# Routing scores of two tiles per strip on VectorE, and four row buffers instead of five

## The chip, the cores and the metric

The kernel runs on one core of one Trainium2 chip. The metric is the device time of one launch in microseconds (us). Three runs of the kernel before gave 1011.37, 1012.25 and 1013.17 us, so the median is 1012.25 us. The profile comes from one further execution, which took 1011.34 us; the span that the profile covers in it is 1009.5 us.

The engines of a core work side by side, each through its own instructions in order: TensorE (PE in the profile; PEld is its weight load) multiplies matrices into PSUM, VectorE (DVE) and ScalarE (ACT) work elementwise, GpSimd (POOL) here mostly issues DMAs, and SyncE (SP) issues DMAs from a queue of its own. An engine waits for another through semaphores. SBUF is the memory that the engines work from.

## The reference, cut to what matters

One layer of a graph network over 3125 nodes with 256 features: a layer norm, a GNN branch with sparse products, an attention-like mix, and then a mixture of eight experts with one expert for each node. What the change touches is the routing: the second layer norm's output times an 8-column matrix, from which each node's expert is picked.

```python
xn = _layernorm(x, axis=-1)
x = x + gnn(xn, ...) + mix(xn, ...)
h = _layernorm(x, axis=-1)
logits = h @ gate_w + gate_b          # [3125, 256] @ [256, 8]
idx = argmax(softmax(logits))
pos = rank of the node among those with the same idx
buf[idx, pos] = h                     # 489 slots for each expert
y = relu(buf @ w1 + b1) @ w2 + b2     # then back to the nodes
out = x + y * probability
```

The GNN branch is `h = A x`, then `z = A h` and a softmax, then `A` times that result and a second softmax. `A` is the sparse 3125 x 3125 matrix, which the kernel builds as a dense one in HBM (`adj`).

## The kernel before

**Stages.** The first stage builds `adj` from the edge lists (until about 248 us). Then come three dense products with it: the first with the normed input (two column halves, until about 515 us), the second with `g` (until about 682 us), the third with `late`, the softmax of the second (until about 831 us). Behind the third product come the experts (until about 1001 us).

**The products.** Each product runs over seven strips of target nodes, `STRIPS`: five of four tiles (512 columns), one of three (384) and one of two (181 real columns). A strip takes 25 chunks of source nodes, one matmul each per column half (`multiply`, L275; fp32, so that the trace has two records for one matmul). The chunks' rows come from HBM in loads of five chunks, 1280 KB for a strip of 512 columns. `load_part` (L250) takes a buffer `at` from `apool` (L772, five buffers of 10 KB per partition) and issues the load on SyncE's queue; so a load waits until TensorE is done with the buffer that it takes over, and SyncE's later instructions wait behind it.

**The strip's tail.** In the third product, TensorE's order is written by hand (L1436 to L1482). While strip s+1 is multiplied, `tail(s)` (L1285), a generator, is advanced between the loads' stretches of five chunks, at the places 0, 2, 3 and 4 of `at` in L1440:

- place 0: the strip's sum is copied (ACT), turned by `w1T` (L1306, PE). Then VectorE and ScalarE do the second softmax, tanh and the sum `x` (L1313 to L1337); the sum lies in `rows`, whose first half is the lower 128 features (done earlier) and the other half the upper 128.
- place 2: TensorE transposes the upper half of each tile (L1343), ScalarE copies the result to `xT` (L1344).
- place 3: TensorE multiplies each turned tile by the upper half of the gate, `gate_c[:, 1, :]`, 8 columns (L1348).
- place 4: VectorE has computed the layer norm's mean and scale (L1353 to L1358, `inv_sqrt` at L115 with three Newton steps), the logits (L1360, sum of TensorE's result and `g_lo`), the choice `oh` (L1372 to L1376) and the running counts `run` (L1379). TensorE then ranks the nodes with two matmuls on `run` and `oh` (L1383, L1384). These stand in TensorE's order ahead of the next strip's chunks.

After that VectorE computes the row numbers (L1398 to L1402), GpSimd scatters the tokens to `xbuf` (L1411) and SyncE writes `x` to `out` (L1424). After strip 3's tail `early_experts` (L1077) picks the two fullest experts, which begin before the last strips are through; their numbers are read by SyncE and GpSimd (L1105, L1459).

**The lower half of the gate** is done on VectorE already, beside the second product: `gate_lo` (L956) holds the gate's rows, spread over all partitions, less their mean; `gate_tile` (L968) multiplies a tile by it into `dot` (L970, 128 x 1024 elements) and sums over the features into `g_lo` (L973). `spread_gate` (L959) loads the rows by a DMA on GpSimd's queue and subtracts the mean (L963).

**Memory.** Pools are laid out as stacks from both ends of SBUF, and a tile that takes over the place of an older one waits for that one's last readers. `hT` (L775, 25 KB per partition, the first product's result) lies above `apool`, and the tiles of the tails come down from the other end as far as its place. TensorE's last reads of `hT` are the transposes at L1013 at the end of the second product. All engines but TensorE in the third product, and all of them in the second, are in the order that the scheduler gives when it builds the program.

Of the kernel before, what the change touches and what calls it, by code (L numbers as in the profile page):

```python
# [8 lines left out]
FP = mybir.dt.float32  # L9
# [3 lines left out]
ALU = mybir.AluOpType  # L13
AX = mybir.AxisListType
PSUM = bass.MemoryType.PSUM

P = 128
N = 3125
D = 256
HD = 128  # L20
# [5 lines left out]
STRIPS = [(0, 4), (4, 4), (8, 4), (12, 4), (16, 4), (20, 3), (23, 2)]  # L26
# [20 lines left out]
NEXP = 8  # L47
# [21 lines left out]
def rows_all(ap, offset, n):  # L69

    return bass.AP(tensor=ap.tensor, offset=ap.offset + offset, ap=[[0, P], [1, n]])
# [3 lines left out]
def gps_layer(ctx: ExitStack, tc: tile.TileContext, a: dict, out: bass.AP):  # L75
    nc = tc.nc
# [8 lines left out]
    small = ctx.enter_context(tc.tile_pool(name="small", bufs=3))  # L85
# [9 lines left out]
    def mm():  # L95
        mm_pools.append(mm_pools.pop(0))
        return mm_pools[-1].tile([P, SW], FP, tag="mm", name="mm")
# [256 lines left out]
    def network(runs):  # L354

        with ExitStack() as net:
            layer(net, runs)

    def layer(net, runs):
# [409 lines left out]
        gnn = net.enter_context(ExitStack())  # L769
        zpool = gnn.enter_context(tc.tile_pool(name="zpool", bufs=2))  # L770
        parts = gnn.enter_context(ExitStack())
        apool = parts.enter_context(tc.tile_pool(name="apool", bufs=5))  # L772
        held_h = parts.enter_context(ExitStack())
        hold = held_h.enter_context(tc.tile_pool(name="hold", bufs=1))
        hT = hold.tile([P, 2, NP], FP)  # L775
# [8 lines left out]
        if runs:  # L784
# [3 lines left out]
        w0T, w1T, b0, b1, gate_b, gate_c, gate_m, g_lo, ones = (  # L788
            held[x]
            for x in ("w0T", "w1T", "b0", "b1", "gate_b", "gate_c", "gate_m", "g_lo", "ones")  # L790
        )
# [202 lines left out]
        for s, (t0, nt) in enumerate(STRIPS):  # L994
# [12 lines left out]
            for j in range(0, nt, 2):  # L1007
                m = min(2, nt - j)
                t = t0 + j
                pt = mm()  # L1010
# [12 lines left out]
            x = xa[:, t0 : t0 + nt, :HD]  # L1023
# [257 lines left out]
        routing = net.enter_context(ExitStack())  # L1281
        strip = routing.enter_context(tc.tile_pool(name="strip", bufs=2, side="right"))
        rpool = routing.enter_context(tc.tile_pool(name="rpool", bufs=3, side="right"))

        def tail(s, p):  # L1285

            t0, nt = STRIPS[s]
            tiles = slice(t0, t0 + nt)

            def st(tag):  # L1290
                return small.tile([P, 4, NEXP], FP, tag=tag, name=tag)[:, :nt, :]
# [4 lines left out]
            def wide_(v):  # L1296
                return v[:, :, None].to_broadcast([P, nt, NEXP])
# [29 lines left out]
            x = rows[:, :, :D]  # L1327
# [9 lines left out]
            nc.vector.tensor_tensor(x[:, :, HD:], xa[:, tiles, HD:], s1, ALU.add)  # L1337


            xT = strip.tile([P, SW], FP, tag="xT", name="xT")  # L1340
            pt = mm()
            for j in range(nt):
                nc.tensor.transpose(pt[:, j * P : (j + 1) * P], x[:, j, HD:], ident)  # L1343
            nc.scalar.copy(xT[:, : nt * P], pt[:, : nt * P])  # L1344
            yield
            pg = mm()
            for j in range(nt):
                nc.tensor.matmul(  # L1348
                    pg[:, j * NEXP : (j + 1) * NEXP], xT[:, j * P : (j + 1) * P], gate_c[:, 1, :],
                    start=True, stop=True,  # L1350
                )
            yield
            mv = small.tile([P, 4, 2], FP, tag="mv", name="mv")[:, :nt, :]  # L1353
            for j in range(nt):
# [3 lines left out]
            inv_sqrt(rs, mv[:, :, 1], nt)  # L1358
            logit = st("logit")
            nc.vector.tensor_tensor(  # L1360
                logit, pg[:, : nt * NEXP].rearrange("p (t e) -> p t e", e=NEXP), g_lo[:, tiles, :],
                ALU.add,
            )
            nc.vector.tensor_tensor(logit, logit, wide_(rs), ALU.mult)
            nc.vector.tensor_tensor(
                logit, logit, gate_b[:, None, :].to_broadcast([P, nt, NEXP]), ALU.add
# [41 lines left out]
            for j in range(nt):  # L1408
                t = t0 + j
# [26 lines left out]
        with tc.manual_schedule(engines={mybir.EngineType.PE}):  # L1436
            behind = iter(())
            end = len(STRIPS) - 1
            for s in range(len(STRIPS)):
                at = (0, 2, 3, 4) if s < end else (0, 4)  # L1440
                (p,) = spmm(
                    s, lambda c, d: s0[:, c, :], 1,
                    lambda i: next(behind, None) if i % (NT // CH) in at else None,
                )
                if s < end:
                    for _ in behind:
                        pass
                    behind = tail(s, p)
                if s == EARLY_AT + 1 and runs:
                    early, num, row, full, low = early_experts()  # L1450
            last = tail(end, p)
            parts.close()
            wts = net.enter_context(tc.tile_pool(name="wts", bufs=2))
# [55 lines left out]
            if runs:  # L1509
# [9 lines left out]
                right = ranked.tile([1, 1], FP, name="right")  # L1519
# [187 lines left out]
```

## Time and profile before

| what | value |
|---|---|
| median of three runs | 1012.25 us |
| the profiled execution | 1011.34 us |
| its span in the profile | 1009.5 us |
| TensorE in the 150 us from 700 to 850 us | busy 149.9 us |
| VectorE there | busy 68.7 us of 150 |
| DMA engines there, in stretches of 50 us | 0.92, 0.90 and 0.94 busy |
| TensorE's clock as granted | 0.993 of full speed on average |

The columns of the profile's tables are explained where they are shown. In a row of instruction groups the duration of one matmul is longer than the time from its start to the next one's start, because matmuls overlap; the chain of waits has the time that each really adds. An engine's idle time before an instruction stands in brackets, with what ended it. The profile marks a queue's own waiting with a q (SPq).

### The profile page before, as it was taken

The numbers are of one execution on the slowest core, as the hardware profiler recorded it, in microseconds if no ns is written. First come the engines' busy times: TensorE is split into PE (matmuls) and PEld (weight loads), VectorE is DVE, ScalarE is ACT, GpSimd is POOL, SyncE is SP. The second block draws the span as 40 slices with busy tenths as digits, with TensorE's granted clock in tenths as the row PEclk, the third lists the DMA queues.
The fourth block names the chain that finished last, engine by engine and source line by source line (L and its number), as shares of the span: only waits on it lengthen the run. The fifth ranks groups of instructions, "written<-read, shape, count | busy, mean of one in ns | idle before, by whom it ended". The sixth has DMA issues, their size and how long they took to land.

```text
span 1009.5 us, 11457 instructions
## 1 busy us (share of the span) xinstructions
PE 977.7 (97%) x4202; PEld 635.9 (63%) x4202; DVE 514.5 (51%) x1149; ACT 304.5 (30%) x567; POOL 98.3 (10%) x113
## 2 busy tenths in 40 slices
PE   5889999999999999999999999999999999999996
PEld 3878888854444444455665554474444578888995
DVE  7999799800343444445653675575444465221211
ACT  3889889830000001001101001110111133224431
POOL 6511000000000000000000000000011142111111
PEclk7999999999999999999999999999999999999999
DMA  4989888993933247421475658769999797713300
GB/s 134 258 240 261 239 238 239 254 263 113 340 116 104 98 139 209 133 75 54 125 243 198 218 196 269 235 182 374 314 310 301 250 320 244 234 36 125 107 30 21
DMA packets 171641, 197.94 MB, mean 196 GB/s; under 512 B 7664, under 2 KB 118304, under 8 KB 171575
## 3 DMA queue, kind: packets, MB, share of 16 engines
q1 hardware_dynamic: 164285, 178.56, 56.6%
q0 software_dynamic: 7248, 18.51, 6.4%
q8 instruction: 35, 0.57, 0.2%
q14 instruction: 31, 0.25, 0.1%
q10 hardware_dynamic: 42, 0.05, 0.0%
HBM read 144.43 MB, written 53.37 MB: 196 GB/s over the span
## 4 chain that ended last, share of the span: by engine, by line
PE 85%; DMA 4%; DVE 4%; ACT 3%; issue 2%; SPq 1%; POOL 0%; POOLq 0%; ACTq 0%; DVEq 0%
PE acc L275 48%; PE mm L1205 7%; PE acc L1162 7%; PE acc L654 5%; PE b L654 5%; PE mm L833 4%; PE mm L889 2%; DMA adj<-st_rows 2%; PE pk L861 1%; ACT st_rows L658 1%; ACT rhs L639 1%; PE mm L916 1%; DMA at<-adj 1%; PE mm L1013 1%; PE mm L1306 1%
## 5 line engine op out<-in xcount | busy, mean ns | idle before, releaser
L275 PE MATMUL acc<-at,xn 128*128 128x512 f32 (+3 forms) x540 | 203.2, 523 | 1.3 <-DMA at<-adj 1.3
L275 PEld LDWEIGHTS acc<-at,xn 128*128 128x128 f32 (+1 forms) x540 | 96.4, 190 | 89.3 <-issue 75.1
L275 PE MATMUL acc<-at,g 128*128 128x512 f32 (+4 forms) x350 | 137.8, 541 | 0.0
L275 PE MATMUL acc<-at,late 128*128 128x512 f32 (+4 forms) x350 | 137.4, 543 | 0.0
L275 PEld LDWEIGHTS acc<-at,late 128*128 128x128 f32 (+1 forms) x350 | 62.4, 190 | 59.6 <-issue 54.1
L275 PEld LDWEIGHTS acc<-at,g 128*128 128x128 f32 (+1 forms) x350 | 62.9, 190 | 58.6 <-issue 52.3
L654 PE MATMUL acc<-rhs,lhs 128*125 128x128 f32 x626 | 85.7, 280 | 9.4 <-ACT rhs L639 8.5
L626 DVE TENSOR_TENSOR lhs<-in_row,in_blk 128x1000 f32<-128x1000 f32 (+1 forms) x79 | 90.3, 1183 | 1.2
L654 PEld LDWEIGHTS acc<-rhs,lhs 128*125 128x125 f32 x626 | 77.5, 191 | 20.9 <-ACT rhs L639 10.2
L654 PE MATMUL b<-rhs,lhs 128*125 128x128 f32 x624 | 81.9, 275 | 0.0
L654 PEld LDWEIGHTS b<-rhs,lhs 128*125 128x125 f32 x624 | 75.4, 190 | 0.0
L639 ACT CAST rhs<-cells 128x2048 f32<-128x2048 bf16 x39 | 74.9, 1920 | 0.2 <-DVE cells L617 0.2
L275 PE MATMUL acc<-a,xn 128*128 128x512 f32 (+1 forms) x160 | 73.1, 595 | 1.2 <-DMA a<-adj 1.1
L846 ACT ACTIVATE sq<-kv 128x512 f32<-128x512 f32 x25 | 15.8, 630 | 179.4 <-DVE kv L842 179.4
L1205 PE MATMUL mm<-w,hm 128*128 128x256 f32 (+2 forms) x288 | 64.3, 380 | 0.0
L839 DVE TENSOR_REDUCE kmean<-mm 128x8 f32<-128x512 f32 x25 | 17.3, 691 | 91.6 <-PE mm L833 91.6
L1162 PE MATMUL acc<-xeT,w 128*128 128x208 f32 (+2 forms) x288 | 58.9, 361 | 1.6 <-ACT hm L1166 0.9
L1205 PEld LDWEIGHTS mm<-w,hm 128*128 128x128 f32 (+2 forms) x288 | 51.2, 180 | 9.6
L1162 PEld LDWEIGHTS acc<-xeT,w 128*128 128x128 f32 x288 | 53.0, 190 | 5.7 <-ACT hm L1166 1.3
L658 ACT COPY st_rows<-acc 125x512 f32<-125x512 f32 (+1 forms) x79 | 47.6, 603 | 25.0 <-issue 14.5
L1166 ACT ACTIVATE hm<-acc,b_e 128x256 f32<-128x256 f32 (+2 forms) x72 | 32.4, 455 | 66.7 <-PE acc L1162 66.5
L617 DVE TENSOR_TENSOR cells<-steps_w,edge_h 128x2048 bf16<-128x2048 bf16 (+1 forms) x40 | 47.7, 1192 | 4.6 <-ACT rhs L639 4.4
(271 smaller groups left out, 1037.8 us busy)
## 6 DMA issues: line engine op xcount, KB each, us to landing
at<-adj SPq DMA_DIRECT2D x52, 1280.0 KB
adj<-st_rows SPq DMA_DIRECT2D x39, 896.0 KB
at<-adj SPq DMA_DIRECT2D x14, 1024.0 KB
at<-adj SPq DMA_DIRECT2D x12, 960.0 KB
w<-in_f_w SPq DMA_DIRECT2D x10, 1024.0 KB
a<-adj SPq DMA_DIRECT2D x39, 256.0 KB
at<-adj SPq DMA_DIRECT2D x12, 452.5 KB
adj<-st_rows SPq DMA_DIRECT2D x39, 104.0 KB
```

The costliest lines, as they stand in the source:

```text
L275: nc.tensor.matmul(ps[d][:, :w], stationary(c, d)[:k], a_rows[:k, :w], start=(c == 0), stop=(c == NT - 1),)
L617: nc.vector.tensor_tensor(cells[:, :m, :, :k], steps_w[:, None, :, :k].to_broadcast([P, m, P, k]), of_pairs(1, g0, ng, P), ALU.is_equal,)
L626: nc.vector.tensor_tensor(lhs[:, j::k], in_row[:, j::k, :, None].to_broadcast([P, m, GR, CA]), in_blk[:, :, None, :, j].to_broadcast([P, m ...
L639: nc.scalar.copy(rhs.rearrange("p (i j) c -> p i j c", j=2), cells.rearrange("p i c j -> p i j c"),)
L654: nc.tensor.matmul(p[:GP, j * P : (j + 1) * P], lhs[:, j0 + j], rhs[:, j0 + j], start=True, stop=True,)
L658: nc.scalar.copy(st[:GP, j0 : j0 + nj, :], p[:GP, : nj * P].rearrange("p (g b) -> p g b", b=P),)
L833: nc.tensor.matmul(pkv, xnT[:, d, t * P : (t + 1) * P], w_kv[:, d, :], start=(d == 0), stop=(d == 1),)
L839: nc.vector.tensor_reduce(mean, p3, AX.X, ALU.add)
L889: nc.tensor.matmul(p[:, j * D : (j + 1) * D], xnT[:, d, (t0 + j) * P : (t0 + j + 1) * P], w_mix[:, d, :], start=(d == 0), stop=(d == 1),)
L1162: nc.tensor.matmul(p[:, :slots], w1[:, d, f * P : (f + 1) * P], xeT[:, d, :slots], start=(d == 0), stop=(d == 1),)
L1166: nc.scalar.activation(hm[:, f, :slots], p[:, :slots], AF.Relu, bias=b1_e[:, f : f + 1], scale=1.0)
L1205: nc.tensor.matmul(p[:n, :D], hm[:, f, c : c + n], w2[:, f, :], start=(f == 0), stop=(f == FC - 1),)
```

## The change

In the first five strips (s from 0 to 4) the last two of the four tiles no longer go through TensorE for the upper half of the gate. VectorE multiplies each of them by `gate_hi`, the upper gate rows spread over all partitions, into a buffer `dot_2`, sums over the features into `part`, and adds that to `g_lo`. TensorE transposes and multiplies the other two tiles only, `xT`'s copy is half as wide, and the logits of two tiles come from PSUM and of two by a copy of `g_lo`. The last two strips keep TensorE for all their tiles.

`gate_hi` and the buffer that holds first the raw rows and then each `dot_2` are two tiles of 4 KB per partition in a new pool; the raw rows (4 KB for each partition, 512 KB) are loaded by one DMA on GpSimd's queue. To make room, `apool` has four buffers instead of five.

```diff
-        apool = parts.enter_context(tc.tile_pool(name="apool", bufs=5))
+        apool = parts.enter_context(tc.tile_pool(name="apool", bufs=4))
...
+        by_rows = routing.enter_context(tc.tile_pool(name="by_rows", bufs=1, side="right"))
+        gate_hi = by_rows.tile([P, NEXP, HD], FP)
+        raw = by_rows.tile([P, HD, NEXP], FP, tag="dot", name="gate_rows_2")
+        nc.gpsimd.dma_start(raw, rows_all(a["gate_w"], HD * NEXP, HD * NEXP).rearrange(
+            "p (d e) -> p d e", e=NEXP))
+        nc.vector.tensor_tensor(
+            gate_hi, raw.rearrange("p d e -> p e d"),
+            gate_m[:, :, None].to_broadcast([P, NEXP, HD]), ALU.subtract,
+        )
...
+            mt = nt - 2 if s < len(STRIPS) - 2 else nt
+            for j in range(mt, nt):
+                dot = by_rows.tile([P, NEXP, HD], FP, tag="dot", name="dot_2")
+                nc.vector.tensor_tensor(
+                    dot, gate_hi, x[:, j, None, HD:].to_broadcast([P, NEXP, HD]), ALU.mult
+                )
+                part = small.tile([P, NEXP], FP, tag="part", name="part")
+                nc.vector.tensor_reduce(part, dot, AX.X, ALU.add)
+                nc.vector.tensor_tensor(g_lo[:, t0 + j, :], g_lo[:, t0 + j, :], part, ALU.add)
             xT = strip.tile([P, SW], FP, tag="xT", name="xT")
             pt = mm()
-            for j in range(nt):
+            for j in range(mt):
                 nc.tensor.transpose(pt[:, j * P : (j + 1) * P], x[:, j, HD:], ident)
-            nc.scalar.copy(xT[:, : nt * P], pt[:, : nt * P])
+            nc.scalar.copy(xT[:, : mt * P], pt[:, : mt * P])
             yield
             pg = mm()
-            for j in range(nt):
+            for j in range(mt):
                 nc.tensor.matmul(
...
             nc.vector.tensor_tensor(
-                logit, pg[:, : nt * NEXP].rearrange("p (t e) -> p t e", e=NEXP), g_lo[:, tiles, :],
-                ALU.add,
-            )
+                logit[:, :mt, :], pg[:, : mt * NEXP].rearrange("p (t e) -> p t e", e=NEXP),
+                g_lo[:, t0 : t0 + mt, :], ALU.add,
+            )
+            if mt < nt:
+                nc.vector.tensor_copy(logit[:, mt:, :], g_lo[:, t0 + mt : t0 + nt, :])
```

What the built program shows of the order: the first product is ordered as before on TensorE. Between the second and the third product, TensorE's order before has one matmul of the third product ahead of the last transposes (L999, L1013); in the changed program that matmul stands behind them. The subtraction into `gate_hi` stands on VectorE between two steps of the second product's last softmax (L140 and L141). In the tails of the strips 0 to 4 the four new large instructions stand on VectorE behind `x` and among the statistics, ahead of `inv_sqrt`. On SyncE's queue the load of each stretch comes one buffer later against TensorE's progress, and the first write of `x` stands one load earlier in the order. GpSimd has one more DMA, ahead of the first tail's work.

## The prediction

> **What bounds the kernel now.** I read the engines' busy times first, then the chain of waits in two tails of the third product, then VectorE's timeline of the last of them, then the stretch between second and third product.
>
> ```profile
> PE 977.7 (97%) x4202; PEld 635.9 (63%) x4202; DVE 514.5 (51%) x1149; ACT 304.5 (30%) x567; POOL 98.3 (10%) x113
> ```
>
> TensorE is busy for 97% of the span, so work taken from it counts one to one where nothing else becomes late. The chain of waits beside strip 1, for the tail of strip 0 (start, length, engine, line, count of records):
>
> ```profile
> 719.05 0.44 PE mm L1343 x4
> 719.49 4.29 PE acc L275 x10
> 723.78 0.79 PE mm L1348 x8
> 724.57 4.59 PE acc L275 x10
> 729.16 0.34 PE mm L1383 x2
> ```
>
> The chain stays on TensorE, which waits for nobody: the tail's small matmuls only take its time. The same in the tail of strip 4, which lies beside strip 5 (384 columns):
>
> ```profile
> 814.16 0.44 PE mm L1343 x4
> 814.60 3.23 PE acc L275 x10
> 817.83 0.79 PE mm L1348 x8
> 818.62 3.52 PE acc L275 x10
> 822.14 0.34 PE mm L1383 x2
> ```
>
> From the transposes to L1383 it is 10.1 us in the first and 8.0 us in the second: VectorE has 2.1 us less there.
>
> **Gain on TensorE.** Half of L1343 (0.44 / 2 = 0.22 us) and half of L1348 (0.79 / 2 = 0.40 us) leave each of five strips: 0.62 us a strip, 3.1 us in all. I take the chain's times, since matmuls overlap and the durations of their group rows would count the overlap too.
>
> **What VectorE gets.** Two multiplies, two sums and two small adds a strip, and a small copy. The lower half of the gate shows the same operation on the same shape:
>
> ```profile
> 679.85 1.22 DVE L970 TENSOR_TENSOR dot<-gate_lo,xa 128x1024 f32<-128x1024 f32 x1
> 681.11 1.22 DVE L973 TENSOR_REDUCE g_lo<-dot 128x8 f32<-128x1024 f32 x1
> ```
>
> The starts are 1.26 us apart, so four cost 4.9 to 5.0 us, and the adds, which go between the statistics, some 0.1 each. From x to the start of the Newton steps (L120) VectorE now takes 1.29 us; with the four it takes about 6.0, or 4.7 more. They stand ahead of L120 in VectorE's order, so the statistics, the Newton steps, the logits, the choice and the counts `run` all queue behind them, and TensorE waits for `run` at L1383, with the next strip's chunks behind it.
>
> *Strips 0 to 3.* In strip 0 x is ready at 716.41 (VectorE's timeline). Plus 6.0, plus 2.4 for the Newton steps, plus the 2.5 from the logits' first step to the last count: `run` at about 727.3. TensorE comes to L1383 at 729.16 less 0.62, or 728.5. So 1.2 us are left, no wait arises, and the gain is whole: 4 x 0.615 = 2.46 us.
>
> *Strip 4.* VectorE's timeline:
>
> ```profile
> 813.04 0.69 DVE L1337 TENSOR_TENSOR rows<-xa,s 128x512 f32<-128x512 f32 x1 [0.75 <-issue]
> ...
> 815.06 0.17 DVE L120 TENSOR_SCALAR nv<-mv 128x4 f32<-128x4 f32 x1
> ...
> 817.47 0.17 DVE L1387 COPY rows<-rs 128x4 f32<-128x4 f32 x1
> ...
> 818.65 0.19 DVE L1360 TENSOR_TENSOR logit<-mm,g_lo 128x32 f32<-128x32 f32 x1 [0.95 <-PE mm L1348]
> 818.88 0.19 DVE L1364 TENSOR_TENSOR logit<-logit,rs 128x32 f32<-128x32 f32 x1
> ...
> 820.72 0.55 DVE L1379 TENSOR_TENSOR run<-run,oh 128x8 f32<-128x8 f32 x3
> ```
>
> Before, VectorE itself waited 0.95 us for TensorE's gate. Now: x ends at 813.77, L120 comes at 813.77 + 6.0 = 819.8, the Newton steps end 817.47 - 815.06 = 2.4 later at 822.2, and from L1364 to the last count before TensorE's ranking is 821.07 - 818.88 = 2.2: `run` at 824.4. TensorE is there at 822.14 - 0.62 = 821.5. It **waits 2.9 us** for VectorE, which becomes the bound at this one place. What is saved in strip 4 goes with it: +2.9 - 0.6 = +2.3 us.
>
> **Does a wait of 2.9 us cost the clock?** What the trace shows of the throttle is the granted clock in 3.4-us windows (window, length, busy PE, PEld, DVE, ACT and POOL, PEclk, DMA share, GB/s):
>
> ```profile
> 9.90:13.30 3.40, 0.41 (x2) 0.20 (x2) 1.65 (x8) 0.34 (x1) 3.09 (x3) 1.00 0.22 43
> 13.30:16.70 3.40, 0.91 (x2) 0.36 (x2) 2.60 (x5) 1.59 (x3) 2.79 (x3) 0.50 0.70 187
> 44.00:47.40 3.40, 1.59 (x15) 1.40 (x14) 3.30 (x8) 3.13 (x4) 3.06 (x2) 1.00 1.06 311
> ```
>
> After a window with TensorE busy for 0.41 us the clock fell to 0.50; after one busy for 1.59 us it stayed at 1.00. The wait, if it fell wholly into one window, would leave 0.5 us of work, near the first row: half clock for at least one window, some 1.7 us. [...] I take 0 for the sum and keep 1.7 as a case.
>
> **Between second and third product.** TensorE before (timeline):
>
> ```profile
> 676.39 6.19 PE L275 MATMUL acc<-at,g 128*128 128x181 f32 x38
> 682.51 1.12 PE L275 MATMUL acc<-at,late 128*128 128x512 f32 x2
> 683.47 0.38 PE L999 MATMUL mm<-ident,zT 128*128 128x128 f32 x2
> 683.69 0.60 PE L1013 MATMUL mm<-ident,hT 128*128 128x128 f32 x4
> 684.12 2.31 PE L275 MATMUL acc<-at,late 128*128 128x512 f32 x5
> ```
>
> One matmul of the third product (0.96 us until L999) filled the wait for `zT`, which ScalarE copies from 682.67 to 683.08. In the new order L999 and L1013 stand ahead of it: TensorE is idle from 682.4 to 683.15, the third product starts at about 683.8 with 25 chunks instead of at 684.12 with 24. A chunk is 0.86 us: 683.8 + 0.86 - 684.12 = **+0.54 us**.
>
> **Four buffers.** The tight place is the same. Loads before were issued at 675.89, 677.81, 679.35, 680.88 and 682.61 and landed at 681.0, 684.4, 687.9, 691.3 and 694.3, 3.4 us apart: the DMA engines are the limit there.
>
> ```profile
> 685.00:690.00 5.00, 5.00 (x13) 2.27 (x12) 4.39 (x11) 0.83 (x2) 0.00 (x0) 1.00 1.05 385
> ...
> 695.00:700.00 5.00, 5.00 (x13) 2.14 (x12) 0.21 (x1) 0.00 (x0) 0.00 (x0) 1.00 1.06 331
> ```
>
> (Columns as in the last fence.) With four buffers the same releases serve one load further back: the third product's first load is issued at 677.81 and lands at 683.0 to 683.4, needed at 683.8; the second at 686.5, needed 688.1; the third at 690.0, needed 692.4; the fourth at 693.5, needed 696.7. No stall, with 0.5 us to spare at the first: from below nothing, from above the 3.4 us of a load that misses its place. I take 0, since landings 3.4 us apart are faster than the 4.3 us that five chunks take. Later in the product three loads are on the way for 12.9 us while one takes 5 to 8 us. The earlier products have the same margin: 0.
>
> **The gate's rows.** The added DMA moves 512 KB to where the share is 1.05: at 385 GB/s that is 1.4 us on the loads behind it (third load at 691.4, still ahead of 692.4). It starts once `hT` is read (L1013, about 684). For its like, L961, issue to VectorE's start took 522.8 - 515.7 = 7.1 us, and the subtraction 2.01, so `gate_hi` is done at 694. VectorE's softmax between L140 and L141 waits for it; TensorE needs that last `late` tile at chunk 23, about 703.6. Nine microseconds of chunks cover it: 0, and without that cover all that is over 9 us. SyncE's first write of x now stands one load earlier and moves it by some 2 us, with 17 to spare; GpSimd's queue is empty there.
>
> **Sum.** -2.46 + 2.3 + 0.54 = +0.4, rounded up to +0.5 for the small adds. On the profiled 1011.34 that is 1011.8; the median lies 0.9 higher, which gives **1012.7 us**. Of this kernel a change of 0.2%, 2.0 us, can be told from none.
>
> **The rivals.**
> *Clock drop after strip 4's wait.* For: the 9.90 row. [...] Price 1.7 less the overlap: +2.0 in all, 1014.2 us.
> *Loads starve.* The other side, slower: with four buffers the first load or the third is late, because the rows for the gate interleave with it ahead of the gap that I assume. It decides from 0.5 us of delay at the first load and 1.0 at the third; from there each load is late by what it lacks, at most 3.4 us for one. For: share 1.05. Against: the landings. +2 to +5, 1013.2 to 1017, middle 1015.
> *VectorE is in time.* The scheduler's order would let the small steps overlap, or x would be ready earlier because TensorE's front part is shorter; if strip 4 waited 0.6 us only, so that it gains nothing, and the boundary lost nothing: -2.46, 1009.8 us. Against: the four instructions alone are 4.9 us against 0.95 of slack and what lies ahead of it.
> *The change does not do what it says*, because the scheduler puts the four behind L120: excluded by the built order.
>
> **How the numbers follow.** Forecast 0.40, clock 0.27, in time 0.17, starving 0.16. The range runs from the third rival's 1009.8 to inside the starving case: 1009.7 to 1016; the likeliest's own is 1011.7 to 1014. Faster by over 0.2% is the third rival, 0.17; slower takes the starving case, the clock case and a little of the forecast's upper end, 0.46; within 0.2% the rest, 0.37.
>
> **What would show it.** L1343 and L1348 at half count in five strips; TensorE idle ahead of L1383 by 2.5 to 3.3 us in strip 4 alone, released by VectorE L1379; PEclk of the next windows; a gap of 0.7 us ahead of L999; no wait of a third-product matmul for `at`. Wrong would be waits at L1383 in strips 0 to 3 (up to 5 x 2 us if x came late), or TensorE idle for loads.

## The result, and the profile after

The changed kernel takes 1017.8 us (median of ten runs, 1016.5 to 1022.08) against 1012.09 us for the kernel before beside it: a ratio of 1.006 (95% interval 1.005 to 1.0071), so **5.7 us slower**. A second measurement on another chip gave 1016.82 against 1013.55, ratio 1.0036 (1.0021 to 1.0052). The prediction was 1012.7 with a range up to 1016.

The profiled execution took 1018.02 us, its span is 1016.4 us. The first row is the page's line of engines, the second its group of the third product's matmuls, whose last part is the idle time just before them and what ended it:

```profile
PE 978.6 (96%) x4172; PEld 636.6 (63%) x4172; DVE 537.8 (53%) x1185; ACT 304.1 (30%) x567; POOL 97.8 (10%) x114
...
L275 PE MATMUL acc<-at,late 128*128 128x512 f32 (+4 forms) x350 | 139.5, 550 | 1.5 <-DMA at<-adj 1.4
```

TensorE has 30 records fewer and yet 0.9 us more of busy time: part of the work ran at a lower clock (0.50 in the windows shown below). And it waited 1.4 us for rows of the matrix, which it had not done before. The view of the waits on TensorE from 680 to 840 us (what waited, for what: sum, times, longest) names all that are new; the same view of the kernel before, from 680 to 835 us, is empty:

```profile
PE mm L1406 <- DVE run L1402: 2.8, 1, 2.8
PE acc L275 <- DMA at<-adj: 1.4, 2, 0.8
PE mm L999 <- ACT zT L983: 0.6, 1, 0.6
```

(L1406 is the ranking that was L1383 before; L1402 was L1379, and L1364, L1369 were L1343, L1348.) Where these stand is seen in TensorE's timelines. From the second to the third product, and to the start of its second strip:

```profile
679.06 6.19 PE L275 MATMUL acc<-at,g 128*128 128x181 f32 x38
685.81 0.44 PE L999 MATMUL mm<-ident,zT 128*128 128x128 f32 x2 [0.57 <-ACT zT L983]
686.09 0.60 PE L1013 MATMUL mm<-ident,hT 128*128 128x128 f32 x4
687.44 21.92 PE L275 MATMUL acc<-at,late 128*128 128x512 f32 x50 [0.75 <-DMA at<-adj]
709.96 4.56 PE L275 MATMUL acc<-at,late 128*128 128x512 f32 x10 [0.60 <-DMA at<-adj]
```

The order is the forecast one, with L999 ahead of the first `late` chunk, but two loads come late. Without the first of them the product would start at 686.69, 1.44 us behind the end of the second (685.25), with 25 chunks to go; before it was 1.54 us (682.58 to 684.12) with 24. One chunk being 0.86 us, the order costs 1.44 + 0.86 - 1.54 = 0.76 us. The start of the first tail (L1306 before, now L1317) gives what this whole stretch loses:

```profile
709.41 1.05 PE L1306 MATMUL mm<-w1T,zT 128*128 128x128 f32 x8
714.35 0.83 PE L1317 MATMUL mm<-w1T,zT 128*128 128x128 f32 x6
```

From the end of the second product it was 26.83 us (709.41 - 682.58) and is 29.10 (714.35 - 685.25). Of the 2.27 us, 0.76 are the order, so late loads cost 1.5. That is more than the 1.35 us of idle time that the two rows show: at the second wait the starts of the matmuls lie 0.75 us further apart than elsewhere and 0.60 are shown as idle, since the matmul ahead is still running by the profile. VectorE's own wait for the gate's rows stands beside it:

```profile
694.72 2.01 DVE L1291 TENSOR_TENSOR gate_hi<-gate_rows,gate_m 128x1024 f32<-128x1024 f32 x1 [3.89 <-DMA gate_rows<-in_gate_w]
```

In strip 4's tail:

```profile
820.09 3.87 PE L275 MATMUL acc<-at,late 128*128 128x384 f32 x10
826.77 0.60 PE L1406 MATMUL mm<-run,ones 128*128 128x32 f32 x2 [2.81 <-DVE run L1402]
827.19 0.61 PE L1407 MATMUL mm<-oh,upto 128*128 128x32 f32 x2
827.62 3.37 PE L275 MATMUL acc<-at,late 128*128 128x181 f32 x10
```

The wait is there. Before, the same ten records of 181 columns took 1.78 us:

```profile
822.54 1.78 PE L275 MATMUL acc<-at,late 128*128 128x181 f32 x10
```

Now they take 3.37: they run at half clock. VectorE's timeline ahead of it, in the changed kernel:

```profile
815.33 0.69 DVE L1348 TENSOR_TENSOR rows<-xa,s 128x512 f32<-128x512 f32 x1 [0.75 <-issue]
816.06 1.23 DVE L1355 TENSOR_TENSOR dot<-gate_hi,rows 128x1024 f32<-128x1024 f32 x1
...
817.40 1.20 DVE L1359 TENSOR_REDUCE part<-dot 128x8 f32<-128x1024 f32 x1
...
820.27 1.21 DVE L1359 TENSOR_REDUCE part<-dot 128x8 f32<-128x1024 f32 x1
...
822.05 0.17 DVE L120 TENSOR_SCALAR nv<-mv 128x4 f32<-128x4 f32 x1
...
826.28 0.55 DVE L1402 TENSOR_TENSOR run<-run,oh 128x8 f32<-128x8 f32 x3
```

From x (816.02) to L120 it is 6.0 us, and VectorE does not pause until `run`. The table by windows (window, length, busy PE, PEld, DVE, ACT, POOL, granted clock, DMA share, GB/s) shows the clock:

```profile
823.00:826.42 3.42, 0.91 (x2) 0.29 (x2) 3.04 (x24) 0.72 (x2) 0.00 (x0) 1.00 1.06 384
826.42:829.83 3.41, 3.06 (x11) 3.09 (x12) 1.04 (x7) 0.00 (x0) 0.26 (x1) 0.50 0.87 275
829.83:833.24 3.41, 3.41 (x14) 3.41 (x14) 0.91 (x2) 0.00 (x0) 2.80 (x3) 0.50 0.37 77
833.24:836.65 3.41, 3.41 (x24) 3.41 (x24) 1.33 (x6) 2.20 (x8) 1.20 (x3) 1.00 0.99 227
```

After a window with TensorE busy for 0.91 us, two windows were at half clock. By this reading half of the busy time in them, (3.06 + 3.41) / 2 = 3.2 us, is lost; e3 measures it.

### The profile page after: what moved, and what is told of

Read it like the earlier page. It is cut to its first block, busy times and chain, and to the rows that moved or that the text cites. A ratio compares the mean times of both kernels' runs of the same rounds, so it can differ in the third digit from the quotient of the medians.

```text
span 1016.4 us, 11441 instructions
## 1 busy us (share of the span) xinstructions
PE 978.6 (96%) x4172; PEld 636.6 (63%) x4172; DVE 537.8 (53%) x1185; ACT 304.1 (30%) x567; POOL 97.8 (10%) x114
## 5 line engine op out<-in xcount | busy, mean ns | idle before, releaser
L275 PE MATMUL acc<-at,xn 128*128 128x512 f32 (+3 forms) x540 | 202.9, 523 | 1.5 <-DMA at<-adj 1.5
L275 PEld LDWEIGHTS acc<-at,xn 128*128 128x128 f32 (+1 forms) x540 | 96.6, 190 | 89.1 <-issue 75.1
L275 PE MATMUL acc<-at,late 128*128 128x512 f32 (+4 forms) x350 | 139.5, 550 | 1.5 <-DMA at<-adj 1.4
L275 PE MATMUL acc<-at,g 128*128 128x512 f32 (+4 forms) x350 | 137.8, 541 | 0.0
L275 PEld LDWEIGHTS acc<-at,late 128*128 128x128 f32 (+1 forms) x350 | 64.6, 196 | 61.7 <-issue 52.5
L275 PEld LDWEIGHTS acc<-at,g 128*128 128x128 f32 (+1 forms) x350 | 62.9, 190 | 58.6 <-issue 52.3
L275 PE MATMUL acc<-a,xn 128*128 128x512 f32 (+1 forms) x160 | 73.1, 595 | 1.7 <-DMA a<-adj 1.6
L1234 DVE SCALAR_TENSOR_TENSOR y<-mm,xe,bx 128x256 f32<-128x256 f32 (+2 forms) x22 | 10.6, 482 | 78.7 <-PE mm L1205 74.3
```

Source lines behind the costliest of these rows:

```text
L275: nc.tensor.matmul(ps[d][:, :w], stationary(c, d)[:k], a_rows[:k, :w], start=(c == 0), stop=(c == NT - 1),)
L1234: nc.vector.scalar_tensor_tensor(y, p[:n, :D], xe[:n, j, D + 2 : D + 3], bx, op0=ALU.mult, op1=ALU.add, accum_out=row_sums[:n, k : k + 1],)
```

## The experiments

**How they are compared.** The first stage, the same in every kernel, ends at times that differ by 4 us from profile to profile. So beside each ratio stands the *third product's length*: from the end of the second product's last matmul to the end of the third's last one, read from TensorE's records of L275. In four kernels whose third product is not slowed (before, e5, e8, e12) it is 148.74 to 148.78 us.

| kernel | ratio to before (95% interval) | first product starts at, us | third product, us |
|---|---|---|---|
| before | 1 | 252.42 | 148.74 |
| changed | 1.0060 (1.0050 to 1.0071) | 255.14 | 153.89 |
| e14, changed again | 1.0036 (1.0021 to 1.0052) | 256.02 | 153.92 |
| e5, before again | 1.0000 (0.9989 to 1.0011) | 253.27 | 148.74 |
| e1, four buffers alone | 1.0071 (1.0054 to 1.0088) | 256.02 | 153.49 |
| e2, strip 4 on TensorE | 1.0047 (1.0029 to 1.0065) | 254.62 | 152.52 |
| e3, wait filled | 1.0037 (1.0021 to 1.0052) | 255.53 | 151.14 |
| e4, last rows split | 1.0037 (1.0024 to 1.0049) | 254.10 | 152.42 |
| e6, weights later | 1.0050 (1.0037 to 1.0063) | 255.35 | 153.98 |
| e7, split and strip 4 on TensorE | 1.0006 (0.9995 to 1.0017) | 254.33 | 148.94 |
| e8, five buffers, split | 1.0000 (0.9990 to 1.0010) | 252.57 | 148.74 |
| e9, fifth's place kept | 1.0071 (1.0050 to 1.0092) | 256.52 | 152.98 |
| e10, four buffers, split | 1.0026 (1.0012 to 1.0041) | 255.26 | 153.11 |
| e11, e7 with later writes | 0.9992 (0.9979 to 1.0004) | 256.38 | 147.96 |
| e12, five buffers, later writes | 0.9999 (0.9981 to 1.0016) | 254.78 | 148.78 |
| e13, five buffers, added matmuls | 1.0021 (1.0003 to 1.0038) | 255.60 | 150.90 |

Both profiles of the changed kernel have a third product 5.2 us longer than before, which lies in both intervals of the ratio (5.1 to 7.2 and 2.1 to 5.3 us).

**e3: is the clock a cost of its own?** Ahead of strip 4's ranking:

```diff
+            if s == len(STRIPS) - 3:
+                pf = mm()
+                for k in range(5):
+                    nc.tensor.matmul(
+                        pf[:, : mt * P], ident, xT[:, : mt * P], start=(k == 0), stop=(k == 4)
+                    )
             p3 = mm()[:, : nt * NEXP].rearrange("p (t e) -> p t e", e=NEXP)
```

> The changed kernel with five matmuls on data at hand (256 columns each, their result is not used) ahead of strip 4's ranking, in the time in which TensorE waits for VectorE. The wait's end is not moved. Theory (the clock is a cost of its own, since TensorE idles 2.5 us of one window): about 0.7 us of idle time are left, the clock stays 1.00, and the kernel is 3.4 us faster than the changed one, about 1014.4. Rival (the clock's fall is incidental or hides behind other work): same time as the changed kernel.

TensorE's timeline:

```profile
824.35 2.43 PE L1408 MATMUL mm<-xT,ident 128*128 128x256 f32 x10
827.43 0.38 PE L1412 MATMUL mm<-run,ones 128*128 128x32 f32 x2 [0.65 <-DVE run L1402]
827.64 0.39 PE L1413 MATMUL mm<-oh,upto 128*128 128x32 f32 x2
827.87 1.78 PE L275 MATMUL acc<-at,late 128*128 128x181 f32 x10
```

The wait's end is where it was against `x`, the granted clock stays 1.00, and the ten records take 1.78 us again. The third product is 2.75 us shorter, although the second strip's first load came 0.47 us later than in the changed kernel (1.07 against 0.60). Together 3.2 us, what the two windows lost. e13 prices the filler where nothing waits: the same five matmuls with five buffers.

> Five buffers and nothing of the change; five matmuls whose result is not used stand ahead of strip 4's ranking. With five buffers, too, the first product starts at 252.4 to 253.3 if the buffers decide, or elsewhere if each program has a start of its own. The time: 2.1 us above before for the added matmuls.

It took 150.90 - 148.74 = 2.16 us more in the third product. So matmuls that cost 2.2 us elsewhere bring 2.75 us here: the clock's loss is shown.

**e2: strip 4 left on TensorE.**

```diff
-            mt = nt - 2 if s < len(STRIPS) - 2 else nt
+            mt = nt - 2 if s < len(STRIPS) - 3 else nt
```

> The changed kernel, with strip 4 left wholly on TensorE (VectorE's part in strips 0 to 3 only). Theory (the wait of 2.8 us in strip 4 and two windows of half clock behind it are the largest loss): no wait ahead of L1406, clock 1.00 through the third product, 2.8 + 3.4 - 0.7 = 5.5 us faster than the changed kernel, so about 1012.3 and the same as before. Rival (buffers and loads are the larger loss): 2 us faster than the changed kernel at most, about 1016.

The third product is 1.4 us shorter, not 5.5; the ratio is that of the rival. The wait ahead of the ranking is gone, but another one stood behind it. TensorE's timeline:

```profile
823.83 0.41 PE L1406 MATMUL mm<-run,ones 128*128 128x32 f32 x2
824.08 0.39 PE L1407 MATMUL mm<-oh,upto 128*128 128x32 f32 x2
826.71 3.14 PE L275 MATMUL acc<-at,late 128*128 128x181 f32 x10 [2.24 <-DMA at<-adj]
```

The last strip's first load is 2.24 us late, and one window of half clock follows. In the changed kernel VectorE's wait lay over it, and both ended together: the ranking started at 826.77, and the trace's semaphore records have the last step of that load at 826.85. **Two causes, each enough to stop TensorE at this place.**

**e1: four buffers alone.**

```diff
-        apool = parts.enter_context(tc.tile_pool(name="apool", bufs=5))
+        apool = parts.enter_context(tc.tile_pool(name="apool", bufs=4))
```

> The kernel before with four row buffers and nothing else of the change. Theory (a load lands only when the slowest of its 16 parts has landed, and four buffers give no room for that): TensorE waits about 0.6 us ahead of L999, 0.7 us for the first load of the third product and 0.6 us for the first load of its second strip, so +2.2 us against before. Rival (the prediction's: only the order at the boundary costs): +0.5 us and no wait for at in the third product. Rival (four buffers cost nothing, all is in the tails): 0.

It loses 4.8 us in the third product, more than either view expected: the last strip's first chunk waits 1.79 us, with a window of half clock behind it (1.7 us), and the boundary costs the rest. The second strip's wait for rows is in neither e1 nor e9; where the gate's rows are loaded too and the last rows are not split (see e4), four of five profiles have it (0.41 to 1.07 us). Why the last strip's first load is late is seen on SyncE's queue and GpSimd's. Before, with five buffers (SyncE):

```profile
806.85 4.48 SPq L259 DMA_DIRECT2D at<-adj  x2
813.76 0.38 SPq L1424 DMA_DIRECT2D out<-rows  x1
```

and GpSimd, with the first MB of the early expert's weights:

```profile
809.83 0.77 POOL L1071 DMA_DIRECT2D w<-in_f_w  x1
```

The last strip's first load (806.85) is ahead of the weights. In e2, on SyncE and then on GpSimd:

```profile
809.02 0.40 SPq L264 DMA_DIRECT2D at<-adj  x1
812.73 0.37 SPq L259 DMA_DIRECT2D at<-adj  x1
815.52 0.38 SPq L1447 DMA_DIRECT2D out<-rows  x1
```

```profile
811.58 0.77 POOL L1071 DMA_DIRECT2D w<-in_f_w  x1
```

The load waits for its buffer until 812.73, is behind 2 MB of weights, and TensorE gets the 452 KB 14 us after the issue.

**e6: the weights issued behind the expert's rows.**

```diff
-            early = [expert_weights(of_pool(wts_0), nc.gpsimd, e), None]
+            early = [None, None]
...
                     early[r] = [early[r], xe, HALF, space_0]
+                early[0][0] = expert_weights(of_pool(wts_0), nc.gpsimd, e)
```

> Strip 4 on TensorE as in e2, and the loads of the first early expert's weights (2 MB on GpSimd's queue) issued behind that expert's rows, some 7 us later. Theory (with four buffers the first load of the last strip is issued behind these weights and not ahead of them, and lands 14 us after its issue): the 2.2 us of waiting at the last strip's first chunk and the window of half clock behind it go, 3.9 us faster than e2, about 1012.0. Rival (the load is late for its own late issue alone): the wait stays, and the time is that of e2, 1015.9.

The first load is in time now, so the weights did hold it. But the kernel gains nothing, since a later load of the same strip is held instead:

```profile
827.12 3.23 PE L275 MATMUL acc<-at,late 128*128 128x181 f32 x20
834.53 3.68 PE L275 MATMUL acc<-at,late 128*128 128x181 f32 x13 [4.17 <-DMA at<-adj]
```

The expectation of a gain was wrong. From 813 to 820 us the DMA engines are now only 0.73 busy (1.00 in e2), and the weights, issued at 821.12, stand ahead of the load that is issued at 824.47 and lands at 834.49.

**e4: the last 53 rows of a strip as 48 and 5.** The trace's semaphore records have 16 steps for one load, as many as the page counts DMA engines. In the changed kernel the load for the second strip has 15 of them by 706.05 and the last at 709.91; TensorE starts at 709.96. The third product's first load has 14 by 686.42, the last at 687.40, and TensorE starts at 687.44. The load of the last 53 rows (L264, 106 KB) has a single step when it lands, beside one at its issue. By an estimate from the 385 GB/s that 16 engines moved, one moves 24 GB/s and takes 4.5 us for 106 KB; the lag at the second strip is 3.9. Where such a load is the last on its way, in the changed kernel's first product from 349.30 to 353.20 us, the DMA engines are 0.07 busy and move 25 GB/s, about one of 16. The single step agrees with that, and so do the two parts in e4: the load of 48 rows has 16 steps and that of 5 rows has 5.

```diff
         if full < CH:
-            held["last_load"] = nc.sync.dma_start(
-                at[:LAST, full, :w], adj_rows[r0 + full * P : N, c0 : c0 + w]
-            )
+            even = LAST // 16 * 16
+            r1 = r0 + full * P
+            nc.sync.dma_start(at[:even, full, :w], adj_rows[r1 : r1 + even, c0 : c0 + w])
+            held["last_load"] = nc.sync.dma_start(
+                at[even:LAST, full, :w], adj_rows[r1 + even : N, c0 : c0 + w]
+            )
```

> The changed kernel, with the load of a strip's last 53 rows divided into one of 48 rows and one of 5. Theory (the 53 rows go over a single DMA engine, 106 KB at its share of the rate being some 4 us, and this engine's part of every later load is late by as much): the 16 parts of a load land within 1 us of each other, the waits for at at the start of the third product (0.75 us) and at its second strip (0.60 us) go, 1.4 us faster than the changed kernel. Rival (the lag comes of the gate's rows or of code loading): the parts are apart as before, and the time is the same.

The steps of a load around the second strip now lie 1.2 to 2.0 us apart, not within 1 us, but the lag of 4 is gone, and so are the waits (TensorE's waits, 680 to 835 us):

```profile
PE mm L1409 <- DVE run L1405: 3.0, 1, 3.0
PE mm L1002 <- ACT zT L986: 0.6, 1, 0.6
PE acc L278 <- DMA at<-adj: 0.2, 1, 0.2
```

The third product is 1.47 us shorter than in the changed kernel. 1.17 of it stand ahead of the first tail (27.94 us from the end of the second product, not 29.10); the other 0.3 go with the clock, since the two windows at half clock held 5.86 us of work and not 6.47.

**e8: the same split with five buffers.**

> The kernel before with its five buffers, and the last 53 rows loaded as 48 and 5. Theory (the lagging engine is there before the change as well, the fifth buffer hides it): the 16 parts of a load land within 1 us of each other, and the time is that of before within 0.2%. Rival (the lag costs there too): over 2 us faster.

No difference: 148.74 us. Before, too, one engine ran 4.4 us behind (a load of the second strip had 15 steps by 699.58, the last at 704.03), and the fifth buffer covered it.

**e10 and e7: the split without and with VectorE's part.** e10 is e1 with the split, e7 is the changed kernel with the split and e2's line.

> Four buffers without VectorE's part, the last 53 rows loaded as 48 and 5. Theory (e1 loses 1.8 us at the last strip's first chunk, 1.7 to the clock behind it and 0.8 to the slower start of the third product, most of it through the lagging engine): at most 0.7 us of waiting at the last strip, clock 1.00, 3 to 4 us faster than e1, about 1015; and slower than e7 by the 2.7 us that VectorE's four strips save. Rival (the lag is no cause): the time of e1.

> Four buffers, VectorE's part in strips 0 to 3 only, and the last 53 rows loaded as 48 and 5. Theory (single-engine loads are what makes four buffers too few at the start of the third product and most of it at the last strip): no wait for at from 680 us on or one under 1 us, clock 1.00, about 1011 to 1012. Rival (the weights alone hold the last strip's first load): a wait of 1.5 to 2.2 us there with a window of half clock, about 1014.

e10 still waits 1.05 us at the last strip and 0.63 at the start, and the clock still fell, so it gains only 0.4 us in the third product over e1. At the last strip the split took 0.74 us of e1's 1.79, against the expectation. It did not take the lag away there: the steps of e10's load lie from 823.47 to 827.42. How much of this wait is the lag is therefore not settled; between e2 and e7 the first chunk's wait fell by 1.55 of 2.24. e7 waits 0.69 and 0.58 us there, keeps its clock, and is level with before. It is 4.2 us shorter than e10 in the third product: 2.7 from the four strips, 0.3 at the start, and 1.2 at the end, where e10 lost 1.7 to a window of half clock and e7 waited longer.

**e11: e7 with two writes moved.** The writes of x of strips 3 and 4 are gathered and issued after the last load:

```diff
+            if s in (3, 4):
+                writes.append(write)
+            else:
+                write()
...
             last = tail(end, p)
+            for write in writes:
+                write()
```

> e7 with the writes of x of strips 3 and 4 (512 KB each) issued behind the last load of the third product. Theory (what is left of the last strip's waits in e7, 0.69 and 0.58 us, comes of the write that stands ahead of its loads): these waits go, 1.3 us faster than e7, 1010.4. Rival (the weights alone): the waits stay, same as e7 or slower by what the later writes delay.

```profile
PE acc L278 <- DMA at<-adj: 0.9, 2, 0.5
PE mm L1002 <- ACT zT L986: 0.6, 1, 0.6
```

At the last strip 0.37 us of waiting are left. The third product takes 147.96 us, 0.8 less than before, the only kernel that is shorter there; the device time, at 0.9992 (0.9979 to 1.0004), can't be told from before.

**e5, e9, e12, e14: the first stage.** The first five profiles with four buffers started the first product 1.7 to 3.6 us later than the one of before.

> The kernel before, unchanged, for a second profile. All five profiles with four buffers have the first product start at 254.1 to 256.0 us, the one of before at 252.4. If that is the spread of the first stage, this one starts the product anywhere from 252 to 256 us, and the same time as before is measured; if the change costs 2 us there, it starts at 252.4 again.

> Four buffers alone as in e1, with the place of the fifth kept free, so that hT and the zero rows for xbuf lie where they lay before. Seven profiles with four buffers start the first product at 254.1 to 256.0 us, three with five buffers at 252.4 to 253.3. Theory (the places of these two tiles change the first stage's transfers): 252.4 to 253.3 here, and 2 us faster than e1, about 1016.7. Rival (the place is not it): 254 or later, and the time of e1, 1018.7.

> Five buffers, nothing on VectorE, the writes of x of strips 3 and 4 behind the last load of the third product. The instructions of the first stage are those of before. If the first stage's time goes with the number of buffers, the first product starts at 252.4 to 253.3; if it goes with each program anew, anywhere from 252 to 256. The time: that of before within 0.2%, moved by the first stage alone, since no load is late with five buffers.

> The changed kernel, for a second profile. Theory: the first product starts again at 254 us or later; one wait of 2.8 us ahead of strip 4's ranking and two windows of half clock behind it; waits for at of 0.6 to 0.8 us at the start of the third product and of 0.6 to 1.1 at its second strip; 1017.8 us. If the first stage is mere spread, the start is anywhere from 252 to 256.

The place of the fifth buffer is not it (e9: 256.52). With five buffers e12 and e13 start at 254.78 and 255.60, in the midst of the others. So the spread of the first stage explains it. In the eleven kernels with four buffers the loss of the median lies from 1.7 us below to 2.9 above that of the third product, 0.5 above on average: an effect of the change on the first stage is not seen, but a small one is not excluded. e14 repeats the wait ahead of the ranking (3.0 us) and the two windows. Its waits for rows are shown as two of 0.33 us, neither at the second strip, but the first tail starts as late as in the changed kernel: 29.20 us behind the second product, not 29.10.

## Why the prediction was wrong, point by point

The steps of the sum, in the third product:

| step | forecast, us | measured in the changed kernel, us |
|---|---|---|
| halves of the small matmuls, strips 0 to 3 | -2.46 | -2.66 (24.52 to 23.86 for a strip) |
| strip 4, net | +2.3 | +2.15 (2.81 less 0.66) |
| clock after the wait | 0 | +3.2 |
| order at the boundary | +0.54 | +0.76 |
| late loads (four buffers, and the gate's rows) | 0 and 0 | +1.5 (1.6 in e14) |
| sum | +0.4 | +4.95 of 5.15 |

**Right:** the gain of a strip, the 6.0 us on VectorE, no wait in strips 0 to 3, the wait of strip 4 (2.9 forecast, 2.8 and 3.0 measured), the order at the boundary, and that VectorE's wait for the gate's rows (3.89 us) reaches TensorE nowhere.

**Wrong, the largest term:** the step on the clock. No run shows the 0 that the sum takes for it; in its place e3 showed 3.2 us. The 0 was the author's estimate: a wait of 2.9 us lies wholly in one window of 3.4 us only if it starts in its first 0.5 us. It need not be wholly in one. By the rows at hand the clock stayed at 1.00 after 1.8 us of idle time in a window (3.40 - 1.59) and fell to 0.50 after 3.0 (3.40 - 0.41); what lies between was open, and the step took the strict end. In the changed kernel one window had 2.5 us of idle time (3.42 - 0.91), and the next two were at 0.50. If 2.05 us are enough (see the last section), a wait of 2.9 us loses the clock from about two thirds of its possible starts in a window, by estimate. The price is nearly twice the 1.7 of the rival, because two windows followed. The rival had the mechanism; its size and its chance of 0.27 were too small.

**Wrong, the second term:** "No stall" for four buffers, and the 0 for the gate's rows. The landings were taken too early. In the kernel before, the steps of the first five loads of the third product begin within 0.3 us of the landings that the prediction gives (681.0 to 694.3), and the last of their 16 steps comes 1.2 to 1.7 us after them. In the changed kernel the first load was issued as forecast, 4.77 us ahead of the second product's end. Against that end the first four loads landed 1.3 to 3.2 us later than forecast, so the margin of 0.5 to 1 us was not there. What late loads cost, by the start of the first tail (less 26.83 us and the 0.76 of the order), depends on two things:

| late loads ahead of the first tail, us | last 53 rows in one load | as 48 and 5 |
|---|---|---|
| four buffers alone | 0.4 and 0.6 (e1, e9) | 0.7 (e10) |
| with the gate's rows too | 1.3 to 1.9 (changed, e2, e3, e6, e14) | 0.4 to 0.6 (e4, e7, e11) |

So four buffers cost about 0.5 us, and the gate's rows on top of the single-engine lag another 1; the split takes that away. No kernel loads the gate's rows with nothing else of the change, so their share is read from this comparison alone. The rival "Loads starve" had the mechanism ("because the rows for the gate interleave with it"); its lower end of 1013.2 us is +1, not the +2 that it names.

**Missed:** "Later in the product three loads are on the way for 12.9 us while one takes 5 to 8 us" was read in the middle of the product and carried to its end, where the early expert's weights take the DMA engines and a load takes 14 us. e2 shows this wait of 2.24 us. It is not in the changed kernel's sum, because VectorE's wait lies over it; it is why the repair of strip 4 alone brings 1.4 us.

The 0.2 us between the sum and the 5.15 is not assigned. That the median moved by 5.7 and 3.3 us in two measurements fits the spread of the first stage.

## What to carry to other kernels

- A wait of TensorE costs its length and can cost the clock behind it (3.2 us by e3). Where a new wait leaves TensorE idle for some 1.8 us or more of a 3.4-us window (here the clock fell each time from 2.05 us on, and went either way from 1.79 to 1.95), put the windows at half clock into the sum, and ask what could fill it; 2.2 us of matmuls that nobody needs brought 2.75 us here.
- Read a load's landing from its slowest part. The 53-row DMA went over one engine (a single step, 25 GB/s), and with the DMA engines busy (1.04 from 700 to 710 us) a load behind it had its last step 3.9 us after the 15th (4.4 before); the lag was free (e8) until the spare buffer was taken away and the gate's rows came on top.
- Before a prefetch is shortened, look at each place where other transfers start (behind 2 MB of weights a load took 14 us in e2); and where a wait is removed, look for the one that lies under it (e2), since the time is that of the later of the two.

## What the runs showed of the hardware

*The clock fell after windows in which TensorE was busy for 1.36 and 1.48 us.* Over the 16 profiles, from 20 us on, in windows of 3.41 us (laid out from the times at which the granted clock changed): all with TensorE idle for 2.05 us or more were followed by half clock (14 of them), and 1.36 us of work in one (e4) did not prevent it. From 1.79 to 1.95 us of idle time it went either way: before kept its clock after 1.50 us of work (54.30:57.70), and the changed kernel lost it in its first stage after 1.48:

```profile
55.00:58.42 3.42, 1.48 (x13) 1.28 (x13) 3.42 (x5) 3.42 (x5) 0.00 (x0) 1.00 0.95 262
58.42:61.83 3.41, 3.41 (x17) 3.41 (x18) 3.34 (x5) 2.80 (x5) 0.00 (x0) 0.50 0.98 277
```

Below 1.79 us it fell once, after 1.05 us in e10 at the last strip. How a wait lies in the windows seems to count too: e1 and e9 have the same wait at the last strip (1.79 and 1.75 us); in e1 it falls into one window and costs the clock, in e9 it is divided between two (0.87 and 0.88) and does not. That is one pair, in the range where it went either way.

*Half clock lasted longer where the wait ran on into it.* Between 20 and 1000 us the 16 profiles have 20 spells of half clock. In all five that lasted two windows (changed, e14, e4, and one each in the first stage of e10 and e13) TensorE was still idle for 0.35 to 2.12 us of the first one. In 14 of the 15 that lasted one window it was busy throughout; the exception is e6, idle for 0.49 us. In the changed kernel the wait ran 0.35 us on into the first window at half clock. No run varied this alone, so the reason stays open.
